# A two-layer graph network on one Trainium2 core: an order of its own for pairs without layer 1, one norm piece per pair, and weight tiles made by GpSimd at the end

## Chip, cores and metric

The kernel runs on one core of a Trainium2 chip. The metric is device time in microseconds; before the change three runs gave 3794.14, 3798.22 and 3801.02, median 3798.22. Engines are named as in the profile: PE (TensorE, the matrix engine; PEld its weight loads), DVE (VectorE), ACT (ScalarE), POOL (GpSimd) and SP (SyncE, which here only issues DMAs). Each engine works through its own instructions in the order of the program and waits at the first one that isn't ready.

## What is computed

x is 8 x 2048 x 256, adj 2048 x 2048 with between one and two per cent of ones. Per batch b, layer 0 is attention whose softmax runs over chunks of 256 keys apart and sums the eight results; layer 1 is a graph attention whose scores are a sum of a source and a target term.

```python
def layer0(x):                       # 4 heads of 64
    q, k, v = x @ Wq.T + bq, x @ Wk.T + bk, x @ Wv.T + bv
    s = clip(q @ k.T / 8, -10, 10)   # per head
    s = where(adj == 0, -10, s)
    ctx = sum over 8 key chunks of softmax(s[chunk]) @ v[chunk]
    return layernorm(ctx @ Wo.T + bo + x) * gamma + beta
x1 = layernorm(x + layer0(x))
def layer1(h):                       # 4 heads of 64
    Wh = h @ W
    e = leaky_relu(src[i] + dst[j], 0.2) where adj[i, j] else -inf
    return elu(softmax(e, over j) @ Wh)
out = layernorm(x1 + layer1(x1))
```

## The kernel before

**Stages.** The eight batches run one after another. Batch b's layer 0 is a loop over 32 pairs of slots; a slot is one chunk of 512 queries (`q`, four of them), one half of the heads (`hp`) and one chunk of 256 keys (`c`). Layer 1 of batch b - 1 runs *along* with the pairs of batch b, four weight tiles a pair. Batch 0 has nothing to run along, so its 32 pairs are plain; it turns the adjacency into masks on the way (`Masks.step`, 48 pieces). In batch 7 layer 1 of batch 6 runs along up to pair 22, the last nine pairs are plain, and 18 steps are kept for the work after the pairs. Layer 1 of batch 7 runs alone at the end, 64 steps of two tiles. Between two batches lies a turnover: the last query group of the old batch is finished and the next batch is projected, by a list of closures called `order`.

**A pair** (loop over `p`; `i` is the pair within its query chunk, 0 to 7). `burst(p + 1)` issues the scores of the next pair (PE, L394, four units of 128 x 1024) and evicts the first (DVE, L406: clip and mask from PSUM into a tile with the tag `pr`); the second eviction follows at once. Then `product(s0)` (PE L440) and a copy of its result (ACT L447), `normalize(s0)` (reciprocal on DVE L457, multiply and add on POOL L464 and L466), evictions three and four, and `product(s1)`. The exponentials (ACT L429) work in place in the `pr` tiles, and the products of the next turn read them. The pool of `pr` has six buffers. Scores, products, projections and outputs take their PSUM in turn from three tiles of two banks, `psA0` to `psA2`.

**Along.** `Layer1.make` makes a weight tile (DVE L783: row of source factors, maximum with a target factor, times the edge tile; all three in SBUF), `use` multiplies it on PE (L805, 32 instructions of 128 x 65) into `psL0` and `psL1`. Eight units of 16 tiles; at a unit's end ACT copies the sums (L817) and `close` normalizes them in pieces, taken by `rest`, into `h1` (L845). Rows come by DMA from `rowD` (L754), where `rows` in `factors` has stored them; edge tiles from `edgeD` (L765, four buffers).

**Around a pair.** The tables `FIRST_OF`, `MIDDLE_OF`, `ON_ACT`, `END_OF`, `LAST_OF` and their `NEXT_` twins say, by `i`, which piece of work on the previous query group (class `Between`: output projection, two layer norms, projection for layer 1) is done at which place of the pair. Norms are sums and squares on ACT (L524, L536), factors on DVE and POOL (L548 to L551), and the application on ACT (L555). `CLOSING` is the same by pair for the final norm of layer 1 of batch b - 2 (class `Close`), `CLOSING_ALONE` and `ENDING` by step in the last stage.

**Homes.** x of the next batch's groups (`project.load`) lies in two buffers `xb`, which the residual of `Between` uses as well.

Of the kernel before, what the change touches and what calls it, by code (L numbers as in the profile page):

```python
# [17 lines left out]
P = 128  # L18
# [4 lines left out]
def adj_resnorm_kernel(  # L23
# [55 lines left out]
    AHEAD_E = 3  # L79
    n_banks = WIDE // QT  # L80
# [235 lines left out]
    def project(b, g):  # L316
# [5 lines left out]
        def load():  # L322
            st["x"] = load_turned(x, b, g, "xp") if b else load_x(b, g, "xp")
# [240 lines left out]
    class Between:  # L564
# [91 lines left out]
        1: lambda o: o.bias(),  # L656
        4: lambda o: o.shift(),
        7: lambda o: o.scale(),
    }
    ON_ACT = {  # L660
        3: lambda o: o.a.sums((0, 1)),
        4: lambda o: o.a.sums((2, 3)),
        5: lambda o: (o.a.squares(every), o.a.factors()),
        6: lambda o: o.a.apply(o.y),
    }
    END_OF = {
        7: lambda o: o.again(),
# [5 lines left out]
    NEXT_FIRST = {3: lambda o: o.load()}  # L673
    NEXT_MIDDLE = {4: lambda o: o.turn()}
    NEXT_ON_ACT = {
        0: lambda o: o.b2.sums(every),
        1: lambda o: (o.b2.squares(every), o.b2.factors()),
        2: lambda o: o.finish(),
# [60 lines left out]
    class Layer1:  # L739
        def __init__(self, b, gd, waug):  # L740
            self.b, self.gd, self.waug = b, gd, waug
            self.made = self.used = 0
            self.rows, self.edge, self.e = {}, {}, {}
            self.tail = []
            for k in range(AHEAD_E):
                self.load_edge(k)
            self.load_row(0)
# [22 lines left out]
        def make(self):  # L770
# [8 lines left out]
            if j % JG == 0:  # L779
                self.load_edge(k // JG + AHEAD_E)  # L780
            w = BANKS[m] * P
            e = ep.tile([P, WIDE * P], F32, tag="e", name="e")
            nc.vector.scalar_tensor_tensor(  # L783
                e[:, :w],
                self.rows[n][:, :w],
# [6 lines left out]
            self.made += 1  # L792

        def use(self):
# [3 lines left out]
            if j == 0:  # L798
                self.pa = [
                    psL.tile([P, QT, D1], F32, tag=f"psL{i}", name="pa") for i in range(n_banks)  # L800
                ]
# [58 lines left out]
    class Close:  # L860


        def __init__(self, b, g, home):
            self.b, self.g = b, g
            self.h = h1[:, QT * g : QT * (g + 1), :]
            pool, tag, bufs = home
            self.x = pool.tile([P, QT, F], F32, tag=tag, name="x1g", bufs=bufs)
# [50 lines left out]
    HOME_PR = (prp, "pr", 6)  # L918

    class Closing:  # L920
# [5 lines left out]
        def do(self, s, *kinds):  # L926
            for g, step, *more in self.table.get(s, ()):
                if step not in kinds:
                    continue
                if step == "load":  # L930
                    self.of[g] = Close(self.b, g, *more)
# [8 lines left out]
                elif step == "sums":  # L940
                    self.of[g].n.sums((0, 1, 2, 3))
                elif step == "squares":
                    self.of[g].n.squares((0, 1, 2, 3))
                    self.of[g].n.factors()
# [9 lines left out]
    for g in range(NCH):  # L954
# [7 lines left out]
        if g + 2 < NCH:  # L962
            groups[g + 2][0]()
        queries()
        masks.step()
        if g > 1:
            masks.step()
        if g == 1:
            finish_constants()

    CLOSING = {
        -1: [(0, "load", HOME), (1, "load", HOME)],
        0: [(0, "add")],
        1: [(0, "sums"), (1, "add")],
        2: [(0, "squares"), (1, "sums"), (2, "load", HOME_Y)],
        3: [(0, "finish"), (1, "squares")],
        4: [(1, "finish"), (2, "add"), (3, "load", HOME_Y)],
        5: [(2, "sums")],  # L980
        6: [(2, "squares"), (3, "add")],
        7: [(2, "finish")],
        8: [(3, "sums")],
        9: [(3, "squares")],
        10: [(3, "finish")],
    }
    CLOSING_ALONE = {
        -1: [(0, "load", HOME_PR), (1, "load", HOME_PR)],
        1: [(0, "add")],
        2: [(0, "stats"), (1, "add")],  # L990
        3: [(1, "stats")],
        4: [(0, "finish"), (2, "load", HOME_PR)],
        5: [(1, "finish"), (3, "load", HOME_PR)],
        7: [(2, "add")],
        8: [(2, "stats"), (3, "add")],
        9: [(3, "stats")],
        10: [(2, "finish")],
        11: [(3, "finish")],
    }
    ENDING = {  # L1000
        35: [(0, "load", HOME_PR)],
        36: [(1, "load", HOME_PR)],
        37: [(0, "add")],
        38: [(0, "stats")],
        39: [(1, "add")],
        40: [(0, "finish"), (1, "stats")],
        42: [(1, "finish")],
        59: [(2, "load", HOME_PR), (3, "load", HOME_PR)],
        62: [(2, "most")],
        63: [(3, "most")],  # L1010
    }
    lower = None
    for b in range(B):
        waug = blocks.tile([P, NT, H, D1], F32, tag="waug", name="waug")
        sd = small.tile([P, 2 * H, NT], F32, tag="sd", name="sd", bufs=1)
        if b == 0:
# [4 lines left out]
            for us in units_of(0):  # L1021
                exps(*us)
        if lower:
# [6 lines left out]
        for p in range(PAIRS):  # L1030
# [26 lines left out]
            hook(FIRST_OF, NEXT_FIRST)  # L1057
# [13 lines left out]
            elif not lower and masks.left():  # L1071
                masks.step()
            hook(MIDDLE_OF, NEXT_MIDDLE)
            if closing:
                closing.do(p, "add")
# [5 lines left out]
            normalize(s0)  # L1081
            if more:
                for us_ps in waiting[1:]:
                    evict(*us_ps[0], us_ps[1])
            hook(ON_ACT, NEXT_ON_ACT)
            if closing:
                closing.do(p, "sums", "squares", "finish")
# [4 lines left out]
            if more:  # L1092
                exps(*us[2])
            if along:
                along.rest(1)
# [5 lines left out]
            elif not lower and masks.left():  # L1101
# [132 lines left out]
```

## Time and profile before

| | us |
|---|---|
| median of three runs | 3798.22 |
| the profiled execution | 3793.95 |
| its span, first to last instruction | 3792.1 |
| PE busy | 3570.4 (94%) |
| DVE busy | 3079.9 (81%) |
| ACT busy | 2237.4 (59%) |
| POOL busy | 1390.2 (37%) |

Busy time is the union of an engine's instructions, so a PE that is 94% busy isn't at its peak. The stages follow each other in the span: projections and first masks to about 79 us, batch 0's pairs to 417, a turnover of some 72 us, batch 1's pairs from 489 to 860, and so on to batch 7's pairs, 3159 to 3520; the work after them to 3596; layer 1 alone to 3777; and a tail to 3792. The largest waits that end on one engine's work are POOL's for the reciprocal (1401.4 us in 397 times), ACT's for products (578.6), ACT's for evictions (386.8) and DVE's for the copies of products (234.2); POOL is idle most of the time and its waits cost nothing by themselves.

### The profile page before, as it was taken

The page shows a single profiled execution, that of the slowest core. Times are in us where ns is not written, and L with a number is a line of the kernel's source. Part 1 is how long each engine was busy: PE and PEld are TensorE (multiplying, and loading weights), DVE is VectorE, ACT ScalarE, POOL GpSimd, SP SyncE. Part 2 cuts the span into 40 slices and gives each one's busy share as a digit, 9 for nine tenths or more (in the row PEclk, how much of TensorE's full clock was granted, in tenths as well). Part 3 has the DMA queues.
Part 4 walks back from the last instruction along what each step waited for, and adds up shares of the span by engine and source line. Part 5 has one row for each costly group of instructions (what it writes and reads, how often), then busy time and mean ns, then how long its engine had stood idle before and what let it go on. Part 6 is the DMA issues. An engine that isn't in the chain of part 4 may idle for free.

```text
span 3792.1 us, 168780 instructions
## 1 busy us (share of the span) xinstructions
PE 3570.4 (94%) x76884; PEld 2632.2 (69%) x76884; DVE 3079.9 (81%) x3701; ACT 2237.4 (59%) x4083; POOL 1390.2 (37%) x1202
## 2 busy tenths in 40 slices
PE   8888899999999999999999999999999999998787
PEld 4555577776777767776677767777677776775676
DVE  4765489995999869996899959998699977996799
ACT  4676455664766656665666647666576656666222
POOL 0444234342443434432444424444244433444300
PEclk9999999999999999999999999999999999999899
DMA  6652333434433334433434434333444334442354
GB/s 161 148 113 52 68 93 99 106 95 98 126 104 105 84 108 115 109 106 79 119 106 108 103 84 123 104 103 89 105 125 109 103 83 120 109 108 63 90 149 137
DMA packets 635261, 399.02 MB, mean 105 GB/s; under 512 B 423216, under 2 KB 521904, under 8 KB 634544
## 3 DMA queue, kind: packets, MB, share of 16 engines
q1 hardware_dynamic: 584544, 354.53, 36.7%
q10 hardware_dynamic: 50000, 33.70, 2.9%
q8 instruction: 601, 9.85, 1.1%
q14 instruction: 116, 0.95, 0.1%
HBM read 331.22 MB, written 56.89 MB: 102 GB/s over the span
## 4 chain that ended last, share of the span: by engine, by line
PE 78%; DVE 13%; issue 5%; ACT 3%; DMA 1%; POOL 0%; DVEq 0%; ACTq 0%; SPq 0%; POOLq 0%
PE pc L440 23%; PE ps L394 21%; PE pa L805 19%; PE pp L339 6%; DVE pr L406 4%; DVE e L783 4%; PE pw L633 3%; PE po L591 3%; PE pv L355 2%; ACT raw L447 1%; ACT junk L536 1%; DVE y L611 1%; DMA slab<-clipD 0%; DVE xg L579 0%; ACT y L555 0%
## 5 line engine op out<-in xcount | busy, mean ns | idle before, releaser
L429 ACT ACTIVATE pr<-pr 128x1024 f32<-128x1024 f32 x1024 | 1078.5, 1057 | 421.3 <-DVE pr L406 386.8
L783 DVE SCALAR_TENSOR_TENSOR e<-srow,gd,et 128x1024 f32<-128x1024 f32 x1024 | 1304.1, 1311 | 20.5 <-PE pa L805 11.2
L406 DVE SCALAR_TENSOR_TENSOR pr<-ps,slab 128x1024 f32<-128x1024 f32 x1024 | 1187.9, 1202 | 98.5 <-PE ps L394 90.7
L805 PEld LDWEIGHTS pa<-waug,e 128*64 128x64 f32 x32768 | 1016.1, 139 | 234.0 <-issue 171.2
L440 PE MATMUL pc<-vaug,pr 128*64 128x65 f32 x32768 | 1060.2, 223 | 81.9 <-DVE pr L406 79.8
L805 PE MATMUL pa<-waug,e 128*64 128x65 f32 x32768 | 1081.2, 224 | 44.3 <-DVE e L783 38.5
L440 PEld LDWEIGHTS pc<-vaug,pr 128*64 128x64 f32 x32768 | 1011.0, 139 | 110.6 <-DVE pr L406 103.8
L464 POOL TENSOR_TENSOR part<-raw,rd 128x512 f32<-128x512 f32 x448 | 481.0, 1074 | 1408.0 <-DVE rd L457 1401.4
L394 PE MATMUL ps<-qT,kT 64*64 64x512 f32 x8192 | 954.7, 599 | 27.3 <-DVE pr L406 22.8
L447 ACT COPY raw<-pc 128x520 f32<-128x520 f32 x512 | 302.8, 591 | 581.0 <-PE pc L440 578.6
L394 PEld LDWEIGHTS ps<-qT,kT 64*64 64x64 f32 x8192 | 279.8, 132 | 524.8 <-issue 267.6
L466 POOL TENSOR_TENSOR acc<-acc,part 128x512 f32<-128x512 f32 x448 | 581.0, 1297 | 35.2
L457 DVE RECIPROCAL rd<-raw 128x8 f32<-128x8 f32 x512 | 99.9, 195 | 240.0 <-ACT raw L447 234.2
L464 POOL TENSOR_TENSOR acc<-raw,rd 128x512 f32<-128x512 f32 x64 | 66.8, 1044 | 379.7 <-DVE rd L457 379.7
L339 PE MATMUL pp<-xT,wk_sb 128*128 128x512 f32 x256 | 128.4, 649 | 28.4 <-DVE xT L301 25.7
L837 ACT ACTIVATE sums<-sums,dn 128x64 f32<-128x64 f32 x504 | 131.7, 334 | 15.5 <-DVE dn L831 12.3
L633 PE MATMUL pw<-w_sb,x1T 128*64 128x264 f32 (+1 forms) x800 | 126.8, 395 | 4.0 <-DVE x1T L301 4.0
L591 PE MATMUL po<-wo_sb,qT 128*64 128x256 f32 (+1 forms) x912 | 123.0, 386 | 0.0
L355 PE MATMUL pv<-wv_sb,xT 128*128 128x256 f32 x512 | 115.9, 379 | 0.0
L339 PE MATMUL pp<-xT,wq_sb 128*128 128x512 f32 x256 | 115.9, 595 | 0.0
L339 PEld LDWEIGHTS pp<-xT,wk_sb 128*128 128x128 f32 x256 | 51.2, 208 | 92.2 <-issue 56.3
L817 ACT COPY sums<-pa 128x260 f32<-128x260 f32 x126 | 41.9, 369 | 115.1 <-PE pa L805 113.6
(125 smaller groups left out, 2107.3 us busy)
## 6 DMA issues: line engine op xcount, KB each, us to landing
et<-edgeD SPq DMA_DIRECT2D x512, 256.0 KB, 2.9
slab<-clipD SPq DMA_DIRECT2D x256, 256.0 KB, 3.5
srow<-rowD SPq DMA_DIRECT2D x64, 512.0 KB, 4.4
xg<-in_x_dram SPq DMA_DIRECT2D x32, 512.0 KB, 4.9
x1D<-y ACTq DMA_DIRECT2D x32, 512.0 KB, 3.3
x1g<-x1D SPq DMA_DIRECT2D x32, 512.0 KB, 5.8
out_dram<-x1g SPq DMA_DIRECT2D x30, 512.0 KB, 3.5
ctxD<-acc ACTq DMA_DIRECT2D x56, 256.0 KB, 2.8
```

The lines of the kernel that those rows point to most:

```text
L339: nc.tensor.matmul(pps[c], lhsT=w[:, kc, c * P : (c + 1) * P], rhs=st["xT"][:, kc, :], start=(kc == 0), stop=(kc == KC - 1),)
L394: nc.tensor.matmul(ps[z * D : (z + 1) * D, k, :], lhsT=kT[rows, hp, t * P + z * D : t * P + (z + 1) * D], rhs=qT[rows, hp, cols], start=Tr ...
L406: nc.vector.scalar_tensor_tensor(pr, ps, -CLIP, row.unsqueeze(1).to_broadcast([P, 2, CH]), op0=ALU.max, op1=ALU.min,)
L429: nc.scalar.activation(pr, pr, AF.Exp, scale=0.125)
L440: nc.tensor.matmul(pc[z * D : (z + 1) * D, k, to], lhsT=probs[s][u][:, k, i * P + z * D : i * P + (z + 1) * D], rhs=vaug[:, KT * c + u, 2 ...
L447: nc.scalar.copy(raws[s].rearrange("p k i d -> p k (i d)"), pc[:, :, : QT * D1])
L464: nc.gpsimd.tensor_mul(part, raw[:, :, :, :D], rd.to_broadcast([P, 2, QT, D]))
L466: nc.gpsimd.tensor_add(accv, accv, part)
L591: nc.tensor.matmul(po[z, k, :], lhsT=qT[:, c, t * P + z.start : t * P + z.stop], rhs=wo_sb[:, c, :], start=(c == 0), stop=(c == KC - 1),)
L633: nc.tensor.matmul(pw[z, k, : F + 2 * H], lhsT=self.x1T[:, c, u * P + z.start : u * P + z.stop], rhs=w1_sb[:, c, :], start=(c == 0), stop= ...
L783: nc.vector.scalar_tensor_tensor(e[:, :w], self.rows[n][:, :w], self.gd[:, h, j : j + 1], self.edge[k // JG][:, j % JG, :w], op0=ALU.max, ...
L805: nc.tensor.matmul(self.pa[i // QT][z * D : (z + 1) * D, i % QT, :], lhsT=e[:, i * P + z * D : i * P + (z + 1) * D], rhs=self.waug[:, j, h ...
```

## The change

- **Plain pairs** get their own order. The third eviction and third exponential come before the middle hook and `product(s0)`, the fourth eviction and exponential right after the product, and `normalize(s0)` after these. The second mask step of a pair stands after it, and from pair 6 on only in even pairs. In the first projections the slabs, the burst of pair 0 and its exponentials come before the last queries.
- **Norm pieces** on ACT go to the end of the pair, after `product(s1)`, at most one a pair, and the tables are spread anew; the factors become a step of their own.
- **x tiles** of odd groups lie in `pr`; in the last stage the x tiles of `Close` lie in `kT` and `qT`, which nobody reads any more.
- **The turnover's order** is written anew.
- **At the end**, with layer 1 alone, GpSimd makes tiles 3 and 6 of every seven, by a maximum and a product with a bf16 copy of the edge tile that ACT makes; DVE's tiles go to `pr`; ACT copies each unit's row into PSUM (`lift`), and DVE reads it there. The sums of odd units lie in `psA2`. The first row's load is issued five steps before the lone stage.

```diff
 def load():
-    st["x"] = load_turned(x, b, g, "xp") if b else load_x(b, g, "xp")
+    if b == 0:
+        st["x"] = load_x(b, g, "xp")
+    else:
+        t = prp.tile([P, KC, CH], F32, tag="pr", name="xp") if g % 2 else None
+        st["x"] = load_turned(x, b, g, "xp", t)
...
 MIDDLE_OF = {
-    1: lambda o: o.bias(),
-    4: lambda o: o.shift(),
-    7: lambda o: o.scale(),
+    2: lambda o: o.bias(),
+    6: lambda o: (o.a.factors(), o.shift()),
 }
-ON_ACT = {3: sums (0, 1), 4: sums (2, 3), 5: squares and factors, 6: apply}
-END_OF = {7: again}
+FINALLY_OF = {4: sums, 5: squares, 6: apply}
-NEXT_FIRST = {3: load}
-NEXT_MIDDLE = {4: turn}
-NEXT_ON_ACT = {0: b2.sums, 1: b2.squares and factors, 2: finish}
+NEXT_MIDDLE = {0: scale, 1: again, 3: b2.factors, 4: load, 5: turn}
+NEXT_FINALLY = {1: b2.sums, 2: b2.squares, 3: finish}
...
+def by_pool(self, k):
+    return self.alone and k % 7 in (3, 6)
+def lift(self, n):
+    if n < len(UNITS):
+        self.lifted[n] = psA.tile([P, WIDE * P], F32, tag=f"psA{n % 2}", name="rowp")
+        nc.scalar.copy(self.lifted[n], self.rows[n])
+def make_ahead(self, k):
+    while self.begun < min(k + LEAD + 1, TILES):
+        t = self.begun
+        self.begun += 1
+        if not self.by_pool(t):
+            continue
+        n, j = t // NT, t % NT
+        m, h = UNITS[n]
+        mask = blocks.tile([P, WIDE * P], BF16, tag="y", name="mask")
+        nc.scalar.copy(mask, self.edge[t // JG][:, j % JG, :])
+        e = ep.tile([P, WIDE * P], F32, tag="e", name="e")
+        nc.gpsimd.tensor_scalar(e, self.rows[n], self.gd[:, h, j : j + 1], None, ALU.max)
+        nc.gpsimd.tensor_mul(e, e, mask)
+        self.e[t] = e
 def make(self):
...
-    e = ep.tile([P, WIDE * P], F32, tag="e", name="e")
+    self.made += 1
+    if self.alone:
+        if j == NT - LEAD:
+            self.lift(n + 1)
+        self.make_ahead(k)
+        if self.by_pool(k):
+            return
+        e = prp.tile([P, WIDE * P], F32, tag="pr", name="e")
+        row = self.lifted[n]
+    else:
+        e = ep.tile([P, WIDE * P], F32, tag="e", name="e")
+        row = self.rows[n]
...
 # pair loop
     if along:
         along.rest(1); along.make(); along.use(); along.make()
-    elif not lower and masks.left():
-        masks.step()
+    else:
+        if more:
+            evict(*waiting[1][0], waiting[1][1])
+            exps(*us[2])
+        if not lower and masks.left():
+            masks.step()
     hook(MIDDLE_OF, NEXT_MIDDLE)
...
     product(s0)
-    normalize(s0)
-    if more:
-        for us_ps in waiting[1:]:
-            evict(*us_ps[0], us_ps[1])
-    hook(ON_ACT, NEXT_ON_ACT)
+    if along:
+        normalize(s0)
+        if more:
+            for us_ps in waiting[1:]:
+                evict(*us_ps[0], us_ps[1])
+    elif more:
+        evict(*waiting[2][0], waiting[2][1])
+        exps(*us[3])
...
-    elif not lower and masks.left():
-        masks.step()
-    hook(END_OF, {})
+    else:
+        normalize(s0)
+        if not lower and masks.left() and (p < QP - 2 or p % 2 == 0):
+            masks.step()
...
     product(s1)
-    if more:
+    if along and more:
         exps(*us[3])
     hook(LAST_OF, NEXT_LAST)
+    hook(FINALLY_OF, NEXT_FINALLY)
...
 # turnover, b + 1 < B: k, v, q project; l loads x, t turns it; fs are most, spread, rows
-order = [begin, early[0], *rest, l1, k0, early[1], *rest, ctx, v0, steps[0], early[2], *rest]
-order += [steps[1], t1, *rest, q0, steps[2], early[3], steps[3], *rest, k1, l2, steps[4], v1]
-order += [steps[5], q1, early[4], t2, l3, steps[6], k2, early[5], steps[7], early[6], q2]
-order += [steps[8], steps[9], t3, v2]
-order += [lambda: [load_slab(p) for p in range(2)], fs[0], k3, fs[1], fs[2], v3]
-order += [start_next, q3, lambda: [exps(*us) for us in units_of(0)]]
+order = [begin, early[0], *rest, l1, k0, ctx, early[2], v0, steps[0], *rest, steps[1], t1, l2, *rest]
+order += [q0, steps[2], early[3], steps[3], l3, k1, *rest, v1, early[4], t2, steps[4], q1]
+order += [steps[5], k2, early[5], early[6], steps[6], v2, t3, steps[7], k3]
+order += [lambda: [load_slab(p) for p in range(2)], steps[8], steps[9], q2, fs[0], v3, fs[1]]
+order += [start_next, fs[2], q3, lambda: [exps(*us) for us in units_of(0)]]
```

The tables of closures are shortened here to what they call. `CLOSING` changes in the same way: one of add with factors and finish, sums, or squares in each pair from 0 to 11; `CLOSING_ALONE` loads all four groups at once and takes sums and squares on ACT in place of the statistics on DVE.

## The prediction

> **What bounds the kernel now.** I cut the span into stages first, with the busy time in each: the 32 pairs of batch 0 (no layer 1), one batch with layer 1, one turnover between batches, two microseconds after a stall in it, the last nine pairs of batch 7, and the last layer 1, which runs alone.
>
> ```profile
> 79.00:416.00 337.00, 279.25 (x5329) 184.27 (x5326) 218.45 (x290) 218.37 (x328) 141.85 (x127) 0.96 0.45 98
> 1824.00:2195.00 371.00, 365.32 (x9074) 277.55 (x9072) 338.64 (x376) 243.22 (x456) 157.00 (x134) 1.00 0.39 105
> 2199.00:2271.00 72.00, 66.97 (x390) 41.04 (x390) 33.02 (x63) 34.97 (x64) 15.51 (x14) 0.98 0.43 104
> 2227.00:2231.00 4.00, 3.90 (x5) 1.65 (x6) 0.00 (x0) 0.86 (x2) 0.00 (x0) 0.57 0.38 131
> 3432.00:3520.00 88.00, 72.47 (x1415) 49.82 (x1417) 47.88 (x62) 54.26 (x91) 39.61 (x35) 0.94 0.24 59
> 3596.00:3777.00 181.00, 150.21 (x4086) 134.31 (x4082) 177.77 (x219) 44.41 (x120) 13.18 (x12) 0.96 0.51 153
> ```
>
> Columns: length, then busy PE, weight loads, DVE, ACT, POOL, granted clock. TensorE fills the batches with layer 1 (365 of 371). Plain pairs are bound by a loop of waits (PE 82%, nobody full). Alone, VectorE is full (178 of 181) and GpSimd idle. A plain pair, in the timeline (start, duration, instruction, idle before it):
>
> ```profile
> 3436.15 2.36 DVE L406 SCALAR_TENSOR_TENSOR pr<-ps,slab 128x1024 f32<-128x1024 f32 x2 [0.16 <-PE ps L394]
> ...
> 3438.59 2.09 PE L440 MATMUL pc<-vaug,pr 128*64 128x65 f32 x64
> 3440.78 0.59 ACT L447 COPY raw<-pc 128x520 f32<-128x520 f32 x1 [1.12 <-PE pc L440]
> ...
> 3441.52 2.31 DVE L406 SCALAR_TENSOR_TENSOR pr<-ps,slab 128x1024 f32<-128x1024 f32 x2
> ...
> 3442.76 2.09 PE L440 MATMUL pc<-vaug,pr 128*64 128x65 f32 x64 [2.08 <-DVE pr L406]
> ```
>
> Product, copy, reciprocal, third eviction, second product: PE waits 2.08. Then a pair with layer 1 where two norm pieces meet on ACT, a turnover, and what GpSimd costs (source view: min/median/max ns):
>
> ```profile
> 1864.19 0.60 ACT L447 COPY raw<-pc 128x520 f32<-128x520 f32 x1
> ...
> 1864.85 1.09 PE L394 MATMUL ps<-qT,kT 64*64 64x512 f32 x8 [0.55 <-ACT raw L447]
> ```
> ```profile
> 2227.10 5.37 PE L339 MATMUL pp<-xT,wk_sb 128*128 128x512 f32 x8 [3.67 <-DVE xT L301]
> ...
> 2254.99 0.32 SPq L754 DMA_DIRECT2D srow<-rowD  x1
> ```
> ```profile
> L466 POOL TENSOR_TENSOR acc<-acc,part x448: 1264/1282/2324, 85.4 to 3522.7; 128x512 f32<-128x512 f32 x150
> ```
> ```profile
> L406 DVE SCALAR_TENSOR_TENSOR pr<-ps,slab x1024: 1162/1214/1226, 68.8 to 3509.7; 128x1024 f32<-128x1024 f32 x171
> ```
> ```profile
> 3575.82 8.22 DVE L783 SCALAR_TENSOR_TENSOR e<-srow,gd,et 128x1024 f32<-128x1024 f32 x4
> ```
>
> L783 takes 1.28 us as a rule; here, beside four GpSimd multiplies (L730, 10.94 us), 2.06 each. L406, whose first input is in PSUM, never exceeds 1.23 in 1024 runs, though GpSimd works in every pair.
>
> **Start of batch 0.** Today the slabs are asked for at 63.8, land 5 us later, and PE idles 4.3. The change asks at about 57 and does the last queries after the burst. A similar idle stays, but the exponentials hide under 3.65 us of queries: first product at 73.3 by these rows, not 76.6. **-3.**
>
> **Plain pairs.** Take the pair's first score matmul as 0. Scores run to 3.59 (four at 0.90), evictions 1 and 2 from 1.15 to 3.51, product 1 from 3.59, its end seen at 5.78. Now: copy, reciprocal, eviction 3 from 6.52, product 2 at 7.75, next pair at 9.77. The change puts eviction 3 ahead of the product in VectorE's order, yet the tag pr has six buffers: four hold the pair in use, two the first new evictions. The third must wait for the buffer that product 1 reads, so it starts at 5.78: product 2 at 7.02. ScalarE now runs exp 3 (1.06), copy (0.59), exp 4 (1.06), copy one behind the other, and the second copy's reciprocal stands ahead of the next evictions: 9.30 per pair, **-0.5**. But everything placed behind eviction 3 on VectorE is late. A mask step's clip and compare (0.73 + 0.40) end at 8.6; the second step's transposes need them and stand ahead of product 2 on PE: 11.0 in place of 10.16. Bias, scale, again, shift, turn (1.2 each), free today under the wait for the copy, add about 0.7 where no output or value matmuls (1.73) cover them. Summing: 14 pairs with two mask steps +12; pairs with one step 0; hooks about +6 (eight exposed 1.2 us pieces); norm pieces of 2.2 to 2.6 move from between copy and exp 3 to the pair's end, where the next scores hide them, -8 (five such pairs take 11.3 to 11.6 today); pairs with nothing else -2. Batch 0 **+8** (0 to +18), batch 7's nine **-2**.
>
> **Pairs with layer 1.** Copies of a pair's first product lie 11.21 apart where nothing disturbs. Batch 4 takes 370.7 from first to last; 30 x 11.21 + 9.25 for the short last + ten pairs with outputs or values at 1.73 = 362.8, so 7.9 is disturbance, with two norm pieces on ACT in one pair, or scale and again on DVE (2.4 against a slack of 11.21 - 4 x 1.165 - 4 x 1.235 - 0.32 = 1.29). With one piece a pair both causes go. What is left: factors, shift and a context turn in slot 6 (0.3 + 1.2 + 0.7), 0.9 over the slack, and a weight-row close (0.65) on top of a 1.2 hook: about 3. Gain 4 to 5 in five batches, 3 in batches 1 and 7 together: **-24** (0 to -40). ACT does 5.4 + 1.2 + 2.6 of 11.21 per pair, so the norm at the end hides; without that cover it costs the 0.55 shown.
>
> **Seven turnovers.** Group 2's x is loaded earlier, x tiles of odd groups live in pr (no new instruction; eight issues of 5.3 us on SP go ahead of the x1t loads, whose turned tile then has 9 us to spare), and its turn goes before the second norm. That takes away the 3.67 wait, the slow clock behind it (5.37 for what takes 3.60) and 1.36 before the row transpose: 6.8. But the row pieces now stand behind the scores, and the last values ahead. Rows: transpose at 2253.2 in this turnover's time, flat copy, store 1.8, load 4.5: landed 2260.1. VectorE has the first weight tiles ahead of the next evictions, so PE, done with queries at 2257.1 and three scores at 2259.8, waits for the fourth until 2263.9. Layer 1's first matmul comes at 2264.8, not 2267.1. A 4.1 us idle should cost 1.8 of clock again, as the 3.67 did. Net -0.5 to -2.3 each, I take -1: **-7** (+10 to -45).
>
> The Trainium skill ("TensorE: Matmul & The Clock Gate", section "What's actually happening") says that an idle window of about 3.4 us halves the clock. The 0.57 above agrees; by the rule the new wait pays too, and closing the old one alone would bring 5.4.
>
> **Layer 1 alone.** Row and first load come earlier: the start moves from 3598.3 to 3595.5, where VectorE is ready. VectorE keeps 92 of 128 tiles: 92 x 1.18 (L406's pitch, 1.16 to 1.20) = 109. Beside them: six adds 1.2, two shorter ones 0.95, eight closes 0.65, small steps 5.7: 20 to 22. Stats of two groups stay in this, four groups' go to ACT. Each GpSimd tile is a one-input maximum and a product. L464 takes 1.04 for 512 and L730 1.93 for 1024, both with a broadcast operand, so 0.17 is fixed. Product: L466, two full operands, 1.282 for 512, hence 2.17 ns each and 0.17 + 1024 x 2.17 ns = 2.40; not under L730's 1.93. The maximum has no row: not under the memset of identb (0.204 for 128, 0.10 for one: 0.83 ns each, 0.95 in all), not over the strided copy L728 (0.298 for 64 against 0.198 for L518's four: 1.67, 1.8 in all); I take 1.1, nearer a plain stream. 36 x 3.5 = 126, bounds 104 and 151. Six norm factor pairs (L550 and L551, 2.3) add 14. So GpSimd is nearly always busy, and VectorE's 16 operations with two SBUF inputs wait for it, by 1.0 (mean remainder of 1.1 and 2.4), the small ones 0.4: +21. VectorE 152, GpSimd 140 + 7 of waits, PE 128 x 0.935 = 120: VectorE ends it at 3747.5. Masks and lifted rows, 44 copies at 1.05, and norms (4 x 6.8) bring ACT from 44 to some 118 of 152; if it falls behind, GpSimd waits for masks. Four x loads issued at once are 2 us of SP ahead of the edge loads, which have three groups of cover. The tail of 15.1 loses the late adds (1.8): end 3761, **-29** (-6 by the upper GpSimd bound, -50 if nothing waits).
>
> Against this speaks "GPSIMD Engine Reference", section "Engine selection": elementwise work belongs on VectorE, since two-input operations take about twice as long here. Row: 2.40 against 1.18. The same table calls one-input work roughly line rate; the maximum would then be an estimated 0.9 us and the stage 1 us shorter. No run shows it yet.
>
> **Sum.** -3 + 8 - 2 - 24 - 7 - 29 = -57 on the profiled execution's 3793.95 (span 3792.1): 3737, and as the median shown is 4.3 higher, **3738** for a median; own range 3715 to 3765.
>
> **Rivals.** (A) GpSimd sets the end: 4.2 per tile, 151 + 14 + 14 of waits = 179 from 3594, with the tail 25 later than above: 3763 in all. For it: no row for the maximum. 0.14. (B) The turnovers come out clean, the row in time: 45 rather than 7, so 3700. Against: the row's path has 7 us less cover than today. 0.16. (C) Eviction 3 does not wait: product 2 at 5.6, 40 pairs at about 8.2 instead of 9.8, near 3672. Against: six buffers. 0.06. (D) Slower: a row in PSUM does not free VectorE from GpSimd. Then 131 of VectorE and 140 of GpSimd exclude each other, 271 in place of 152: 3857; slower as soon as under 62 of them overlap. For it: L783 beside L730; against: L406's spread, though its scalar is an immediate and this one a column in SBUF. 0.10. No change, if plain pairs and GpSimd both meet their upper bounds: 0.04. Forecast 0.50.
>
> Faster than 0.2% (what a measurement here tells from none): forecast, A, B, C, 0.86; same 0.04; slower 0.10. The range 3698 to 3782 leaves out C, D and a little of the rest.
>
> **What would show it.** Right: third eviction starting as product 1 ends; two-mask pairs near 11; no 3.67 gap, but a wait on rowD's load at each batch start; weight tiles at 1.2 beside GpSimd, stage some 152. Wrong: plain pairs under 9; the lone stage above 180; turnovers 6 shorter.

## The result, and the profile after

The changed kernel takes 3834.95 us (median of 4; 3832.7 to 3835.18) against 3799.62 before (median of 4; 3794.14 to 3804.09): a ratio of 1.0092, 95% interval 1.0075 to 1.011. It is slower by 35 us, where 61 less was forecast. Its profiled span is 3833.3 us, against 3792.1.

The span is cut at the copies of products on ACT (`raw<-pc`), 64 a batch, which both kernels have: a batch lasts from the end of its first such copy to the end of its last, a turnover from there to the next, the lone part from the last copy to the last matmul of layer 1 (so it holds the work after the pairs too). "Untouched" is the spread of a stage over those of the runs below whose edit does not touch it (without the shift run, which is told by itself). Each length is that of one profiled run, so this spread is the noise to hold a change against.

| us | before | after | change | predicted | untouched |
|---|---|---|---|---|---|
| up to the first copy | 79.4 | 77.4 | -2.0 | -3 | 73.6 to 82.0 |
| batch 0 | 337.2 | 341.9 | +4.6 | +8 | 339.8 to 341.9 |
| batches 1 to 6 | 2242.9 | 2238.1 | -4.8 | -24, with the next row | 2238 to 2244 |
| batch 7, pairs along | 273.1 | 276.2 | +3.1 | see above | |
| batch 7, last nine pairs | 88.2 | 78.3 | -9.9 | -2 | |
| seven turnovers | 499.0 | 518.3 | +19.3 | -7 | 515 to 520 |
| lone part | 258.5 | 289.7 | +31.2 | -29, with the tail | 289.2 to 290.8 |
| tail | 13.9 | 13.5 | -0.4 | see above | |

Windows of the kernel after (length, then busy PE, weight loads, DVE, ACT, POOL with counts, granted clock, DMA): batch 0, batch 4, the turnover behind it, four microseconds in that turnover, the last nine pairs, layer 1 alone.

```profile
77.40:419.20 341.80, 280.87 (x5318) 182.78 (x5314) 218.85 (x287) 211.65 (x326) 144.96 (x127) 0.97 0.43 96
1834.20:2206.90 372.70, 367.98 (x9194) 281.74 (x9190) 344.46 (x379) 243.15 (x459) 154.05 (x136) 1.00 0.38 104
2206.90:2280.60 73.70, 68.00 (x382) 42.63 (x384) 33.22 (x63) 34.73 (x63) 14.68 (x14) 0.95 0.43 104
2275.00:2279.00 4.00, 4.00 (x76) 4.00 (x76) 2.91 (x3) 0.19 (x1) 0.00 (x0) 0.50 0.00 1
3451.80:3530.10 78.30, 67.22 (x1361) 44.17 (x1358) 44.92 (x59) 51.77 (x91) 38.90 (x35) 1.00 0.26 66
3613.00:3819.00 206.00, 137.64 (x3944) 132.04 (x3941) 136.07 (x146) 101.18 (x224) 182.80 (x82) 0.91 0.38 123
```

In the last row GpSimd is the full engine (183 of 206) and VectorE has 70 us to spare; before, VectorE was full. In the fourth row TensorE works at half clock though the stall is over. The second row says something about the pairs along: TensorE stands idle for 4.7 us of a whole batch, and before, by the same cut, for 5.7:

```profile
1823.90:2199.30 375.40, 369.72 (x9196) 281.60 (x9191) 342.08 (x379) 244.57 (x459) 160.04 (x136) 1.00 0.39 104
```

**Layer 1 alone.** Instructions by source line (minimum, median, maximum in ns):

```profile
L780 POOL TENSOR_SCALAR e<-srow,gd x36: 2835/2843/3923, 3606.1 to 3811.7; 128x1024 f32<-128x1024 f32 x36
...
L781 POOL TENSOR_TENSOR e<-e,mask x36: 2120/2129/2640, 3609.4 to 3814.6; 128x1024 f32<-128x1024 f32 x36
...
L829 DVE SCALAR_TENSOR_TENSOR e<-rowp,gd,et x92: 1233/1275/1285, 3606.5 to 3810.8; 128x1024 f32<-128x1024 f32 x92
```

The maximum takes 2.84, not 1.1, and the product 2.13, not 2.40: about 5.0 a tile. VectorE's tiles with the row in PSUM never exceed 1.285, though GpSimd runs beside nearly all of them. The timeline (start, duration, idle before) and the waits of that stage (total, times, longest):

```profile
3790.78 2.85 POOL L780 TENSOR_SCALAR e<-srow,gd 128x1024 f32<-128x1024 f32 x1
3790.84 1.05 ACT L778 CAST mask<-et 128x1024 bf16<-128x1024 uint8 x1 [2.36 <-POOL e L781]
...
3793.71 2.12 POOL L781 TENSOR_TENSOR e<-e,mask 128x1024 f32<-128x1024 f32 x1
3795.80 2.84 POOL L780 TENSOR_SCALAR e<-srow,gd 128x1024 f32<-128x1024 f32 x1
3795.88 3.02 PE L858 MATMUL pa<-waug,e 128*64 128x65 f32 x96 [2.00 <-POOL e L781]
...
3797.49 0.17 DVE L883 TENSOR_SCALAR dn<-sums 128x8 f32<-128x8 f32 x1 [6.50 <-ACT sums L870]
```
```profile
PE pa L858 <- POOL e L781: 50.2, 28, 4.0
...
ACT mask L778 <- DMA et<-edgeD: 33.0, 9, 5.9
ACT mask L778 <- POOL e L781: 31.7, 14, 4.9
...
DVE dn L883 <- ACT sums L870: 38.6, 7, 7.8
DVE h L898 <- ACT sums L896: 22.6, 6, 7.5
...
POOL e L781 <- ACT mask L778: 15.9, 6, 4.9
```

Here GpSimd's tiles follow each other without a gap, and in the whole stretch from its first tile to its last, 3606.1 to 3816.7, it is busy for 190 of 211 us. TensorE waits for its tiles, and VectorE waits 61 us for ACT, which closes a weight row late. ACT itself waits for two things while it makes masks: for a mask buffer that GpSimd still reads, and for edge tiles from DMA. So there are two suspects: GpSimd's pace, and the mask copies.

**Turnovers.** The one behind batch 4:

```profile
2263.91 0.32 SPq L789 DMA_DIRECT2D srow<-rowD  x1
2264.27 2.70 SPq L800 DMA_DIRECT2D et<-edgeD  x4
...
2269.35 2.48 DVE L829 SCALAR_TENSOR_TENSOR e<-srow,gd,et 128x1024 f32<-128x1024 f32 x2 [5.71 <-DMA et<-edgeD]
...
2273.02 1.99 PE L399 MATMUL ps<-qT,kT 64*64 64x512 f32 x8 [5.05 <-DVE pr L411]
...
2276.73 3.19 PE L445 MATMUL pc<-vaug,pr 128*64 128x65 f32 x64
```

The wait forecast for the row is there: TensorE stops for 5.05 us. The edge loads, which the kernel before issued ahead of the row, now queue behind it. Afterwards a product takes 3.19 us that takes 2.09 elsewhere.

**Plain pairs.** One without a mask, then one with two mask steps:

```profile
3446.95 2.09 PE L445 MATMUL pc<-vaug,pr 128*64 128x65 f32 x64
3448.96 2.36 DVE L411 SCALAR_TENSOR_TENSOR pr<-ps,slab 128x1024 f32<-128x1024 f32 x2 [2.10 <-PE pc L445]
3450.24 2.09 PE L445 MATMUL pc<-vaug,pr 128*64 128x65 f32 x64 [1.21 <-DVE pr L411]
...
95.49 2.09 PE L445 MATMUL pc<-vaug,pr 128*64 128x65 f32 x64
97.51 1.23 DVE L411 SCALAR_TENSOR_TENSOR pr<-ps,slab 128x1024 f32<-128x1024 f32 x1 [2.48 <-PE pc L445]
98.65 0.82 DVE L253 TENSOR_SCALAR clip<-pm 128x640 int8<-128x640 bf16 x1
...
99.92 0.45 PE L251 MATMUL pm<-identb,ab 128*128 128x128 bf16 x5 [2.34 <-DVE ab L241]
100.30 2.09 PE L445 MATMUL pc<-vaug,pr 128*64 128x65 f32 x64
```

The third eviction starts as the first product ends, so it does wait for that product's buffer. TensorE waits 1.21 in place of 2.08 for the second product; with masks it waits 2.34 for the clip and compare (`ab`) behind the late eviction.

### The profile page after: what moved, and what is told of

It reads as the page before. It is cut to its first block, busy times and chain, and to the rows that moved or that the text cites. A ratio compares the mean times of both kernels' runs of the same rounds, so it can differ in the third digit from the quotient of the medians.

```text
span 3833.3 us, 168890 instructions
## 1 busy us (share of the span) xinstructions
PE 3563.0 (93%) x76884; PEld 2643.4 (69%) x76884; DVE 3062.8 (80%) x3633; ACT 2282.4 (60%) x4191; POOL 1537.3 (40%) x1274
## 4 chain that ended last, share of the span: by engine, by line
PE 69%; DVE 16%; issue 5%; DMA 4%; ACT 3%; POOL 3%; SPq 0%; DVEq 0%; ACTq 0%; POOLq 0%
PE pc L445 20%; PE ps L399 18%; PE pa L858 17%; DVE pr L411 7%; PE pp L344 5%; DVE e L829 4%; PE pw L638 3%; PE po L596 3%; PE pv L360 3%; DMA et<-edgeD 2%; POOL e L780 1%; POOL e L781 1%; DMA slab<-clipD 1%; DVE qT L489 1%; DVE h L898 1%
## 5 line engine op out<-in xcount | busy, mean ns | idle before, releaser
L434 ACT ACTIVATE pr<-pr 128x1024 f32<-128x1024 f32 x1024 | 1065.1, 1055 | 559.9 <-DVE pr L411 490.5
L829 DVE SCALAR_TENSOR_TENSOR e<-srow,gd,et 128x1024 f32<-128x1024 f32 x896 | 1177.0, 1346 | 65.1 <-DMA et<-edgeD 36.4
L858 PE MATMUL pa<-waug,e 128*64 128x65 f32 x32768 | 1080.0, 226 | 86.2 <-POOL e L781 50.2
L471 POOL TENSOR_TENSOR acc<-acc,part 128x512 f32<-128x512 f32 x448 | 596.3, 1331 | 35.1
L344 PE MATMUL pp<-xT,wk_sb 128*128 128x512 f32 x256 | 119.0, 608 | 13.5 <-DVE rd L462 12.2
L829 DVE SCALAR_TENSOR_TENSOR e<-rowp,gd,et 128x1024 f32<-128x1024 f32 x92 | 112.0, 1273 | 3.1 <-PE pa L858 1.4
L780 POOL TENSOR_SCALAR e<-srow,gd 128x1024 f32<-128x1024 f32 x36 | 105.6, 2934 | 7.3 <-PE pa L858 7.3
```

What stands on the lines that cost most here:

```text
L344: nc.tensor.matmul(pps[c], lhsT=w[:, kc, c * P : (c + 1) * P], rhs=st["xT"][:, kc, :], start=(kc == 0), stop=(kc == KC - 1),)
L434: nc.scalar.activation(pr, pr, AF.Exp, scale=0.125)
L471: nc.gpsimd.tensor_add(accv, accv, part)
L829: nc.vector.scalar_tensor_tensor(e[:, :w], row[:, :w], self.gd[:, h, j : j + 1], self.edge[k // JG][:, j % JG, :w], op0=ALU.max, op1=ALU.mult,
L858: nc.tensor.matmul(self.pa[i // QT][z * D : (z + 1) * D, i % QT, :], lhsT=e[:, i * P + z * D : i * P + (z + 1) * D], rhs=self.waug[:, j, h ...
```

## The experiments

Each is the changed kernel with the edit shown. Lengths are those of the stages in the table, and each kernel of experiments 1 to 6 has one run. Line numbers move by two or three where an edit adds or drops lines.

**1. Who makes the last weight tiles.** `lone_all_dve`:

```diff
-            return self.alone and k % 7 in (3, 6)
+            return False
```

> Only edit: in the last layer 1 all 128 weight tiles are made by VectorE again; rows stay in PSUM, everything else is the changed kernel. Theory T (GpSimd's own pace, 2.84 maximum + 2.13 product per tile in the profile after, sets the stage of 289.7 us from the last raw copy to the last layer 1 matmul): the stage falls to 245 to 258, against 258.5 before the change, as the row now comes 2 us earlier and tiles cost 1.18 to 1.24; total near 3800. Rival P (the stage is long because the rows in PSUM or the ports slow VectorE, or ACT's lifted rows come late): the stage stays above 275. Rival N (the norm pieces that were moved there set it): stage also above 275. The turnovers stay at their sum of the changed kernel (19 us over those before) in every theory.

Lone part 252.4, time 3799.2: as the first theory had it. The whole loss at the end comes with GpSimd's tiles; all else that changed there (rows in PSUM, the earlier start, norm pieces on ACT) is worth 6 together against before.

`lone_one_of_seven` keeps `k % 7 == 3` alone.

> Only edit: GpSimd makes one weight tile of seven (18 in all) in the last layer 1, not two. Theory T: GpSimd needs 18 x 5.0 = 90 us and some 25 of norm and waits, so VectorE's 110 tiles set the stage: 110 x 1.20 = 132 and some 40 of adds, closes and waits beside them, so the stage from the last raw copy is some 250 less than 10 to 20: 232 to 248 us, total 3775 to 3795; less than with all tiles on VectorE. Rival P (VectorE is slowed whenever GpSimd works, or GpSimd's masks from ACT are late): the stage lies midway between all on VectorE and the changed kernel's 289.7, at 268 or more.

Lone part 250.2, time 3793.5. That misses the first theory's 232 to 248 and is far from its rival's 268. Eighteen tiles fewer should save VectorE 18 x 1.27 = 23 us, and 2 came of it. ACT waited 54.4 us for edge tiles in its mask copies.

**2. Half of GpSimd's tile at a time.** `lone_max_only` drops the mask copy and the product, so 36 tiles lack their edge mask; `lone_product_only` drops the maximum, so they hold row times mask.

```diff
-                mask = blocks.tile([P, WIDE * P], BF16, tag="y", name="mask")
-                nc.scalar.copy(mask, self.edge[t // JG][:, j % JG, :])
...
-                nc.gpsimd.tensor_mul(e, e, mask)
```
```diff
-                nc.gpsimd.tensor_scalar(e, self.rows[n], self.gd[:, h, j : j + 1], None, ALU.max)
-                nc.gpsimd.tensor_mul(e, e, mask)
+                nc.gpsimd.tensor_mul(e, self.rows[n], mask)
```

> The last layer 1 leaves out the edge mask of the 36 tiles of GpSimd: no mask copies on ACT, no product on GpSimd; the maximum stays. VectorE's 92 tiles are unchanged. GpSimd then has 36 x 2.84 = 102 us of tiles. Theory T (the sum of maximum and product paces the stage): the stage from the last raw copy to the last layer 1 matmul falls from 289.7 to below 250. Rival M (ACT's mask copies stand ahead of the copies that close a weight row, and these hold VectorE: 38.6 + 22.6 us of waits in the profile after): those waits vanish here altogether, and the stage is 235 or less, clearly below the 250 of one tile in seven, which has the masks. Rival P (the maximum itself, a scan of SBUF beside VectorE, slows VectorE's tiles): tiles above 1.3 and the stage above 265.

> The last layer 1 leaves out the maximum of GpSimd's 36 tiles (weight row times mask alone); the mask copies on ACT stay. GpSimd then has 36 x 2.13 = 77 us of tiles, near the lower bound of my prediction for it. Theory T: with GpSimd that fast the stage is VectorE's, 92 x 1.27 = 117 and about 45 beside it after a start near 3596: 230 to 248. Rival M (the mask copies on ACT, which wait for edge tiles, hold the closes of the weight rows however fast GpSimd is): waits of VectorE for ACT stay above 20 us in all and the stage at 248 or more, as with one tile of seven.

The lone part is 229.8 without masks, and 258.9 without the maximum. Waits of the second kernel in that stage:

```profile
DVE dn L882 <- ACT sums L869: 19.4, 6, 6.8
DVE h L897 <- ACT sums L895: 17.3, 8, 7.2
...
ACT mask L778 <- DMA et<-edgeD: 53.4, 18, 7.5
...
POOL e L780 <- ACT mask L778: 83.4, 26, 9.5
```

GpSimd now stands idle for 83 us waiting for masks, and the stage is still as long as before the change: a faster GpSimd alone would not have brought the forecast gain. ACT, in its own order, waits for an edge tile, and the copies that close a weight row wait behind it. Without masks these waits of VectorE fall from 61 to 14 us (not to nothing, as the rival expected), and lone part and tail are 243.3, where the forecast comes to 258.5 + 13.9 - 29 = 243.4. Both suspects are real.

**3. Masks in time, GpSimd still full.** `lone_1_of_4_lead3`: 32 tiles, all odd, so each lies in the later half of its edge load, and made three ahead.

```diff
-    LEAD = 4
+    LEAD = 3
...
-            return self.alone and k % 7 in (3, 6)
+            return self.alone and k % 4 == 3
```

> Only edit of the changed kernel: in the last layer 1 GpSimd makes every fourth tile (32, not 36), all in the later half of their edge load, three tiles ahead in place of four, so masks have twice the cover of their edge loads. Theory T (GpSimd's own pace sets the changed kernel's stage of 289.7): 32 x 5.0 = 160 and 28 of norm factors and waits after its first tile, 76 from the last raw copy: stage 260 to 270, and TensorE waits mostly for GpSimd. Rival M (late mask copies alone set it): with masks in time VectorE sets the stage, 96 x 1.27 = 122 and some 115 before and beside: 235 to 250.

```profile
POOL e L781 <- ACT mask L778: 3.7, 4, 1.6
```

Lone part 257.6, 32.0 less than in the changed kernel, a little under the first theory's range and above its rival's. GpSimd waits 3.7 us for masks in place of 15.9 and has four tiles of 5.0 less: 12.2 + 20 = 32.2, which is the whole difference, although VectorE has four tiles more to make. From its first tile to its last GpSimd is idle for 9 of 180 us, in the changed kernel for 21 of 211. So the end of the changed kernel's stage is GpSimd's: its tiles by far the most, and about 12 us of late masks on top.

**4. The turnovers.** `turn_edges_first` moves the row load of a layer 1 that runs along into `begin`, behind its edge loads; `turn_row_early` stores the row one step earlier. The edit of the second:

```diff
-            order += [start_next, fs[2], q3, lambda: [exps(*us) for us in units_of(0)]]
+            order += [fs[2], start_next, q3, lambda: [exps(*us) for us in units_of(0)]]
```

> Only edit: in the seven turnovers the first four edge loads are issued ahead of the row load, as before the change, in place of behind it. Theory R (the row itself is late, the edges only queue 1 us behind it): each turnover loses 0.5 to 1.5 us, their sum from +19 over the kernel before to between +9 and +16; the wait of TensorE of 5.05 stays over 3.5 and the half clock behind it too. Rival Q (the queue order of edges behind the row is the cause): the wait falls below 2, the half clock goes and the sum returns to about -30 against the kernel before. Lone layer 1 unchanged at 289.7.

> Only edit: in the turnovers the step that builds and stores the weight row is done before the third projection of queries but one step earlier than in the changed kernel, so the row's store is issued some 3.6 us earlier. Theory R (the row's late landing makes TensorE wait 5.05 and that wait costs 3.4 of half clock): wait 1.5 to 2.5, no half clock, 5 to 7 us less per turnover, so the seven fall from +19 to between -15 and -30 against the kernel before, total about 3790. Rival S (scores, evictions or the first product hold the batch start, the row being hidden): under 2 us per turnover, the total within 10 of the changed kernel. Rival C (half clock comes whatever the wait): the wait shrinks by 3.6 but clock near 0.5 remains, 3 to 4 us per turnover.

With the edges first the seven turnovers take 505.6, 12.7 less than in the changed kernel, between what the two theories had (6.6 over the kernel before, where they said 9 to 16 over and 30 under); behind batch 4 the wait is 3.95 and the half clock still comes. With the row early they take 487.3: 31.0 less than in the changed kernel and 11.7 less than before, at 3810.3 in all, short of the -15 to -30 against before and of the 3790 in all. The same place there:

```profile
2252.32 0.32 SPq L789 DMA_DIRECT2D srow<-rowD  x1
...
2261.47 1.09 PE L399 MATMUL ps<-qT,kT 64*64 64x512 f32 x8 [1.29 <-DVE pr L411]
```

The row is asked for 5 us before the scores that follow the queries, not 1.3 (after: 2263.91 and 2265.17); TensorE waits 1.29, and from 2263 on its granted clock is 1.00.

**5. Order and slots.** `plain_own_unmasked` gives pairs that still build masks the old order, `plain_old_order` all plain pairs, and `norms_old_places` puts the old tables of norm pieces back. From the edit of the first (the second has `own = False`):

```diff
+            own = not along and not (lower is None and masks.left())
...
-            else:
-                if more:
-                    evict(*waiting[1][0], waiting[1][1])
-                    exps(*us[2])
+            elif own and more:
+                evict(*waiting[1][0], waiting[1][1])
+                exps(*us[2])
```

> Only edit: the norm pieces, x loads and turns stand again in the slots they had before the change (two pieces in some pairs); orders, turnovers and the last layer 1 are the changed kernel's. Theory N1 (one norm piece per pair saves something, but little): batches 1 to 6 together become 3 to 8 us longer than in the changed kernel. Rival N2 (my prediction's -24 is there and something else in the pairs along eats it): they become 15 us or more longer. Rival N3 (the new slots save nothing): within 2 us. Turnovers: the turn of the next x comes later, so 2 to 4 us longer each. The 32 pairs of batch 0 may change by the norm pieces that lie in them, by up to 5 either way.

> Only edit: the pairs of batch 0 that still build masks go in the old order with the old place of the mask steps; plain pairs without masks keep the own order. Theory O (the own order gains only where nothing stands behind the third eviction, and loses in pairs with mask steps): batch 0 falls from 341.9 to 325 to 333, below the 337.2 of before; the last pairs of batch 7 stay as in the changed kernel (354.5). Rival U (the old order costs the same in masked pairs, the loss is in the norm and hook pieces or the start): batch 0 between 336 and 343.

> Only edit of the changed kernel: all pairs without layer 1 go in the old order, masks in their old place; the norm pieces stay in their new slots. Together with the runs before this tells the order from the slots. Theory O: the own order costs some 17 us in the pairs with masks and gains 0.5 to 0.9 in each pair without, so batch 0 is 328 to 337 here (325.3 with the own order in unmasked pairs only, 341.9 with it everywhere), and batch 7 comes to 358 to 364 (354.5). Rival Q (the own order brings nothing, the new slots of the norm pieces make all of the gain): batch 7 within 2 us of 354.5 and batch 0 at 324 to 327.

| us | batch 0 | its first 14 pairs | its rest | batch 7, last nine |
|---|---|---|---|---|
| old order, old slots (before) | 337.2 | 146.6 | 190.6 | 88.2 |
| old order, new slots | 339.7 | 147.4 | 192.3 | 89.7 |
| own order, old slots | 364.6 | 165.5 | 199.1 | 86.2 |
| own order, new slots (after) | 341.9 | 159.1 | 182.8 | 78.3 |
| own order where no masks are left, new slots | 325.3 | 147.4 | 177.9 | 78.3 |

`plain_own_unmasked` gave what was expected, 3821.5 in all. `plain_old_order` lies 3 and 1 us above its ranges, so the own order brings more than expected where no masks stand in it: 14.4 in the rest of batch 0, 11.4 in the nine pairs. Batch 0 with the old slots missed its expectation by far: +22.7, where 5 either way was said; why was not followed up. Under the old order the new slots are worth nothing (+2.5, +1.5), under the own order 22.7 and 7.9. In the pairs along the old slots give 2240.3 for batches 1 to 6, inside the spread of runs that did not touch them; the turnovers, expected 2 to 4 longer each, became 6.9 shorter in all.

**6. The shift in another pair.** `shift_at_7` moves one hook:

```diff
-        6: lambda o: (o.a.factors(), o.shift()),
+        6: lambda o: o.a.factors(),
+        7: lambda o: o.shift(),
```

> Only edit of the changed kernel: the shift stands in slot 7 of a group's pairs, not in slot 6 beside the factors and the context turn. If the crowded slot 6 (12.5 and 13.4 us where the undisturbed pair takes 11.2) is what ate the gain of one norm item per pair: batches 1 to 6 lose 0.8 to 1.5 us each, some 6 in all. Rival (the slack of a pair is used up wherever the 1.2 us shift stands): within 2 us in all.

Batches 1 to 6 take 2232.4, 5.7 less than in the changed kernel and below every other run, but the turnovers take 522.2 (+3.9) and the lone part 293.5 (+3.8), both above the spread in the table, and the time is 3834.5. Nothing is gained; why the other stages lengthened was not followed up.

**7. The parts together.** Edges first, row early, own order only without masks, and the last tiles three ways: all on VectorE; every eighth on GpSimd; every sixth (`k % 6 == 5`), the last two at a lead of three.

> Four edits of the earlier runs together: edge loads ahead of the row load and the row step one place earlier in the turnovers; the old order for pairs that build masks; all tiles of the last layer 1 on VectorE. If the gains are those of separate stages, they add: from the changed kernel's span 3833 minus 30 (row) minus 3 to 7 (edges, partly the same wait) minus 14 to 17 (masked pairs) minus 37 (lone layer 1) = 3743 to 3749, against 3794 to 3803 before. If the causes overlap (the turnovers' gain is given back in the pairs behind them, say), 3765 or more.

> As the combination with all tiles on VectorE, but GpSimd makes every eighth tile (k mod 8 = 3, 16 tiles) of the last layer 1, three tiles ahead in place of four, so that each mask copy has four VectorE tiles (5.1 us) between the issue of its edge load and itself, where the changed kernel's has two or three (landing takes 3.6). Theory E (mask copies that wait on ACT for edge tiles hold the closes of the weight rows, and through them VectorE): ACT's waits for edge tiles fall from 54 to under 25, VectorE's waits for ACT below 5, stage 235 to 245, against 250.2 with one of seven at a lead of four. Rival B (VectorE's two-input operations beside GpSimd eat the gain whatever the lead): stage 247 to 253 again.

> The same with k mod 6 = 5 (21 tiles, all in the later half of their edge load). GpSimd: 21 x 5.0 = 105 and about 30 of other work, below the stage. Theory E: VectorE saves 5 more tiles of 1.27: stage 230 to 242, 3 to 7 below that of one in eight. Rival B: 247 or more.

> The kernel with GpSimd on one tile of six, again and in rounds: 3731 to 3741 if its one run of 3735.9 stands for it, and within 8 us of the one with one tile of eight (3740.0).

| | time, us | ratio to before, 95% | turnovers | lone part |
|---|---|---|---|---|
| all on VectorE | 3746.0 | 0.9863 (0.9843 to 0.9883) | 484.2 | 252.7 |
| one of eight | 3740.0 | 0.9849 (0.983 to 0.9869) | 483.1 | 245.9 |
| one of six, first run | 3735.9 | | 484.4 | 245.2 |
| one of six, rounds | 3733.6 | 0.9842 (0.9819 to 0.9865) | 484.7 | 243.1 |

The gains add. With masks less late GpSimd's help is worth 7 to 10 us rather than 2; ACT's waits for edge tiles fell from 54.4 to 28.0 with one of eight (25 expected) and VectorE's for ACT from 14.1 to 5.0, and the stage ended 1 us above the expected range there, 3 and 1 above with one of six. The last is 1.6% faster than the kernel before by the ratio above (medians 3733.6 and 3797.0) and 2.6% faster than the changed kernel (3835.0, in other rounds).

## Why the prediction was wrong

**The step that failed is the size of GpSimd's maximum.** "The maximum has no row", and the value was bounded by a memset from below and a strided copy from above, 0.95 to 1.8. It measures 2.84: the bounds came from other operations, and the upper one did not hold. Rival A, GpSimd setting the end, was right in kind. With 5.0 in place of its 4.2 its own sum, 36 x 5.0 + 14 + 14, is 208, and GpSimd's tiles run from 3606.1 to 3816.7, 211, where the prediction had VectorE end a stage of 152 and had named a stage above 180 as the sign of being wrong. That alone would have made A's time 3792, no change; of the 43 us from there to 3835 the other terms make 38. From the forecast's 3738: lone part and tail +60, turnovers +26, pairs along +22, nine plain pairs -8, batch 0 -3, start +1, which is 3836. Two of the prediction's own sums are a little off: -57 on the median of 3798.22 is 3741, not 3738, and an end at 3761 lies 31 before the span's 3792.1, not 29; neither changes the argument.

**A second step would have failed behind it.** The edge loads were said to have "three groups of cover". That holds for VectorE's tiles. A mask is copied four tiles ahead of VectorE, so its load has two or three tiles, 2.5 to 3.8 us, where these loads take 3.5 in the median and up to 8.6. That ACT's copies for GpSimd would stand ahead of the closes of the weight rows was not seen; experiment 2 prices masks and product together at 60 us against the maximum's 31, and these do not add, since either can set the end. Also, VectorE's tile took 1.27, not L406's 1.18: 8 us more.

**Turnovers.** The mechanism was right, row and wait included, and the size wrong. The wait is 5.05, not 4.1, with 1 us of it from edge loads behind the row. The half clock lasts from 2272.4 to 2279.2, 6.8 us at 0.50, and costs about 3.4 rather than 1.8; behind the 3.67 of before it lasted half as long, from 2227.3 to 2230.7. And 1.36 before the first projection, from scale and again standing in the pair before, were left out. Together 0.95 + 1.6 + 1.36 = 3.9, from -1 to the measured +2.8 each. Rival B, clean turnovers, needs the row earlier, and even then gives 2.1 each in the combinations, not 6.4.

**Plain pairs** were right in mechanism: six buffers, third eviction at the product's end, 8.9 to 9.7 without masks (9.3 said), 10.8 to 12.7 with two steps and no output product (11.0 said). The first 14 pairs cost 12.5 more, which only looks like the +12 that was said: that was for pairs with two steps, 14 in the batch, and of the first 14 pairs only ten have two. Of these ten, five are within 0.2 of 11.0, four take 12.4 to 12.7 and one, with an output product, 13.15; the four with one step take 0.3 to 0.5 less than before. Rival C is out. The nine pairs gained 9.9 instead of 2: the -2 is the own order with the old slots (88.2 to 86.2), and the spreading of norm pieces, counted for batch 0, was not counted there.

**Pairs along** were mis-sized. The 7.9 above an undisturbed batch was taken for disturbance that spread pieces would remove. TensorE was idle for 5.7 us of that batch, so that is all there was to win; the other 2.2 lie in time in which TensorE was busy. And 4.7 of idle time stayed where about 3 was forecast, so 1.0 went in place of 4 to 5. Putting the old slots back moves nothing beyond the spread.

**Rival D** is refuted: the PSUM row does keep VectorE's tiles at 1.23 to 1.285 beside GpSimd. The slower side was reached by another way: A at a higher price, with turnovers that lost and pairs along that did not win.

## What to carry over

An operation without a row of its own should be bounded by the dearest near row, and the rival that rests on it priced there too: with two products of 2.40 for a tile, A's sum was 3785. Before an engine is given copies for another, look at what stands behind them in its own order, and count the cover of the loads they read from the copy, not from the old consumer. And a gain from removing disturbance is at most the idle time of the engine that sets the stage, which a window shows directly; what pieces that stand alone in a pair still cost comes off that.

## What the runs showed of the hardware

A maximum of a 128 x 1024 f32 tile with a column took GpSimd 2.84 us, longer than a product of two tiles (f32 and bf16), 2.13. The Trainium skill ("GPSIMD Engine Reference", section "Engine selection") calls one-input work there roughly line rate, and two-input work about twice as slow as on VectorE. The product is near that (VectorE's sum of two such f32 tiles, L929, takes 1.22), the maximum is not, and the measurement decides. VectorE's operations with two inputs in SBUF can stretch beside GpSimd (one L929 took 2.9 us with one tile of seven on GpSimd, and 1.21 with none), while those with one in PSUM, 92 tiles of at most 1.285, did not.

A wait of TensorE at the burst of pair 0 cost the clock in some runs and not in others of the same code there: 2.63, 2.67, 2.87, 2.96 and 3.36 us kept it (eight projections in 3.65), 2.67, 3.15, 3.24 and 3.29 lost it (5.3 to 5.5). So the length of a wait does not decide alone. The clock records of the traces show what does. In each trace the granted clock changes only at times that lie whole multiples of 3.413 us apart, to within 0.003. Where the clock was lost, TensorE had been idle for 2.03 to 2.13 us of one such window (`turn_edges_first`, 59.62 to 63.03: busy 1.34, and at half clock from 63.03 on); where it was kept, for at most 1.9 (`lone_product_only`, 59.37 to 62.79: busy 1.51). The wait of 3.36 was cut into 1.57 and 1.80 by the end of a window. Over all 17 traces, behind the first 10 us, each window at full clock with 2.05 us or more of idle TensorE was followed by half clock, and none with under 1.6 while TensorE still had work. The Trainium skill ("TensorE: Matmul & The Clock Gate", section "What's actually happening") has the clock judged over a free-running window of about 3.4 us, which these times agree with; it puts the slow clock behind at least one idle window, where here 2.05 us of a window were enough, and the measurement decides. Those eight projections alone, 1.6 to 1.9 us longer, are part of the spread of the first copy, 73.6 to 82.0 us.
